# Symmetric attention on one core: the blocks below the diagonal of the diagonal pairs go through VectorE and DRAM, and the diagonal pair moves to the end of its row

## The chip, the core and the metric

The kernel runs on one core of one Trainium2 chip. TensorE (PE in the profile), VectorE (DVE), ScalarE (ACT), GpSimd (POOL) and SyncE (SP, which here only issues DMAs) each work through a list of instructions in order, and 16 DMA engines move data between on-chip memory (SBUF) and DRAM. The metric is the device time of one execution in microseconds.

## What is computed

Layer 0 is attention over the 4096 positions of an image, per batch of four, with 128 channels. `q` is both query and key, and it is scaled by its norms, so the matrix of energies is symmetric:

```python
xs = x.reshape(B, C, h, R, w, R).transpose(0, 1, 3, 5, 2, 4).reshape(B, C * R * R, h, w)
q = xs.reshape(B, C * R * R, hw)                    # 4 x 128 x 4096
energy = jnp.einsum('bci,bcj->bij', q, q)
d = jnp.sqrt(jnp.diagonal(energy, axis1=1, axis2=2))
energy = energy / (d[:, :, None] * d[:, None, :])   # symmetric
attn = jax.nn.softmax(energy, axis=-1)
out = jnp.einsum('bcj,bij->bci', q, attn)
x = gamma * out + xs
```

Layer 1 works on tokens of 128 values: layer norm and a linear attention of 8 heads added to the tokens, then a layer norm, a router, and the two best of 8 experts for each token, added again. Everything is float32.

## The kernel before

**Rows, pairs and blocks.** `attend(b, st)` (L394) does layer 0 of one batch. The 4096 positions are NCH = 8 chunks of CH = 512, each of NJ = 4 blocks of 128. Row `i` takes chunk `i` against the chunks `jc <= i`; this is one pair (jc, i). The order inside a row is written out at L408: the diagonal pair (i, i) first, then 0 to i-1. Only the very last row of the last batch (called `ending`) has another order, and there two pairs are computed twice rather than transposed.

**One tick.** Each block `j` of a pair is a tick: a matmul makes a 128x512 tile `pe` of energies (L510), ScalarE makes `pr = exp(pe)` and the sums of its rows (L513), and two ticks later `values` (L417) multiplies `pr` by the values `qT` and accumulates into the row's one PSUM bank `po`, which ScalarE copies to `o` when the row is complete (L422). The helper `after(n, f)` puts a piece of work n ticks later in every queue.

**The other triangle.** Because exp(energy) is symmetric, the pair (jc, i) also serves chunk jc. For `jc < i` VectorE transposes each `pr` in 32x32 blocks into a tile `F` (L368 in the profile, which is the place where `turn_tick` calls the queued work). `move` (L447) writes `F` to DRAM with one DMA of 1 MB, `bring` (L465) reads it back three ticks later with four DMAs of 256 KB into `G`, in an order that finishes the transposition, and puts `transposed_share` (L370) on the list `late`. From `LAG` = 57 units of the hand-written clock later on, one step of the oldest item is taken per tick (`step_share`): a matmul of `G` into a PSUM bank `pg` (L374), and a ScalarE copy into `junk` for the sums (L379). After four steps VectorE adds `pg` to `o[jc]` (L384). There are three `F`, three `G` and two `pg` buffers.

**The diagonal pair.** For `jc == i` only the blocks on and above the diagonal are computed, so block j has 512-128j columns. The six 128x128 blocks below the diagonal are made by `below` (L425): TensorE transposes three blocks in each of two groups into a PSUM bank `ptd` (L443), ScalarE copies them to `gd` with their sums (L433, three copies), and three further `values` matmuls of 256, 128 and 384 columns go into `po`.

**Order of all other work.** `clock[0]` advances by 8 units for a full tick (two per 128 columns for a narrower one) and by 4 for a step of `late`. Work of other stages is woven in by this clock. The list `timed` holds the preparation of the next batch's chunks (`prep`, L283: input DMAs, TensorE transposes, norms) between given percentages of a batch's clock, which is `UNITS` (L1254). The list `steady` holds layer 1 of the batch (`layer1`), which starts at 84% of its batch and then advances one step per `PACE` = 10 units through the next batch. `close_rows` (L627) begins layer 1 of two chunks when `missing()` says that all their shares have been added. In layer 1, tokens are sorted by expert with indirect DMAs on the POOL queue (`xs<-xn`, L935), multiplied (L995), and gathered again (`yb<-ys`, L1060). SP issues nearly all other DMAs, in order: `blocks<-F` (L460), `G<-blocks` (L468), the loads and stores of layer 1 (L959, L981, L1042), and the inputs (L280).

Of the kernel before, what the change touches and what calls it, by code (L numbers as in the profile page):

```python
# [12 lines left out]
F32 = mybir.dt.float32  # L13
# [3 lines left out]
ALU = mybir.AluOpType  # L17
# [5 lines left out]
def kernel(  # L23
# [10 lines left out]
    expert_b: bass.AP,  # L34
    out: bass.AP,
):

# [242 lines left out]
    def prep(b, kc, st):  # L283

        if b == 0:
            if kc == 0:
                st["all"] = big1.tile([P, 4, 8, HW2, 2], F32, tag="T", name="xx_0")
            xx = st["all"][:, kc]
        else:
            xx = xin.tile([P, 8, HW2, 2], F32, tag="xx", name=f"xx_{b}_{kc}")  # L290
        first = b == 0 and kc == 0
        load_tokens(
            xx.rearrange("p k w r -> p k (w r)"), b, 8 * kc, 8, (nc.sync, nc.scalar if first else nc.sync)
        )
        qT = qpool.tile([P, 2, NJ, P], F32, tag="qT", name=f"qT_{b}_{kc}")
        st.setdefault("qT", {})[2 * kc] = qT[:, 0]
        st["qT"][2 * kc + 1] = qT[:, 1]
        yield
        yield
        yield from idle(1)  # L300

        def load_half(g, pt):
            nc.vector.tensor_copy(
                qT[:, :, 2 * g : 2 * g + 2, :].rearrange("p s j (r c) -> p (j r) s c", c=64),
                pt.rearrange("p (m s c) -> p m s c", s=2, c=64),
            )

        for g in range(2):
            yield
            pt, done = hold(f"ptq_{b}_{kc}_{g}", partial(load_half, g))  # L310
            for jj in range(2):
                for r2 in range(2):
                    k = 4 * g + 2 * jj
                    nc.tensor.transpose(
                        pt[:, ts(2 * jj + r2, P)], xx[:, k : k + 2, :, r2].rearrange("p k w -> p (k w)"), ident
                    )
            yield
            done()
        yield
        yield  # L320
        ss = stat.tile([P, 2 * NJ], F32, tag="ss", name=f"ss_{b}_{kc}")
        rn = stat.tile([P, 2 * NJ, 1], F32, tag="rn", name=f"rn_{b}_{kc}")
        for s in range(2):
            sq = work.tile([P, NJ, P], F32, tag="qs", name=f"sq_{b}_{kc}_{s}", bufs=2)
            nc.vector.tensor_tensor(sq, qT[:, s], qT[:, s], ALU.mult)
            nc.vector.tensor_reduce(ss[:, ts(s, NJ)], sq, AX.X, ALU.add)  # L326
            if first:
                pow_neg_half(rn[:, ts(s, NJ), 0], ss[:, ts(s, NJ)])
            elif s == 1:
                pow_neg_half(rn[:, :, 0], ss)  # L330
            yield
            yield
        yield from idle(1)
        if first:
            keep_running(22, ps_g, "pg")
        scaled = []
        for s in range(2):
            qs = work.tile([P, NJ, P], F32, tag="qs", name=f"qs_{b}_{kc}_{s}", bufs=2)
            nc.vector.tensor_tensor(qs, qT[:, s], rn[:, ts(s, NJ)].to_broadcast([P, NJ, P]), ALU.mult)
            scaled.append(qs)  # L340
        for s, qs in enumerate(scaled):
            yield
            qn = npool.tile([P, CH], F32, tag="qn", name=f"qn_{b}_{2 * kc + s}")
            st.setdefault("qn", {})[2 * kc + s] = qn
            pt, done = hold(f"ptn_{b}_{kc}_{s}", lambda p, qn=qn: nc.scalar.activation(qn, p, AF.Copy))
            for j in range(NJ):
                nc.tensor.transpose(pt[:, ts(j, P)], qs[:, j, :], ident)
            yield
            done()
        yield  # L350
        yield
# [5 lines left out]
    LAG = 57  # L357
    exps = []

    def after(ticks, f):  # L360
        queued.append((tick[0] + ticks, f))

# [7 lines left out]
    def transposed_share(b, st, i, jc, G):  # L370

        pg = ps_g.tile([P, CH], F32, tag="pg", name=f"pg_{b}_{i}_{jc}")
        for ib in range(NJ):
# [11 lines left out]
                st["got"][jc] += 1  # L385
            yield "done" if ib == NJ - 1 else None

    def step_share():
        if late and late[0][0] <= clock[0]:
            clock[0] += NJ  # L390
            if next(late[0][1], "done") == "done":
                late.pop(0)

    def attend(b, st):  # L394
# [10 lines left out]

        for i in range(NCH):
            ending = b == B - 1 and i == NCH - 1
            order = list(range(i - 1)) + [i, i - 1] if ending else [i] + list(range(i))  # L408
            twice = (i - 2, i - 1) if ending else ()
            row = {"left": NJ * (i + 1) + NJ - 1}  # L410

            def values(w, blk, lo, hi, i=i, row=row):
                start = "po" not in row
# [51 lines left out]
            def bring(blocks, i, jc):  # L465
# [4 lines left out]
                    )  # L470
                late.append((clock[0] + LAG, transposed_share(b, st, i, jc, G)))

            def back(w, j, jc, i=i):

                if j == 0:
                    while len(held) > 1:
                        held[0]()
                    banks[0] = 2
                    row["back"] = psum_t(f"back_{b}_{jc}")
                nc.tensor.matmul(row["back"], qT[i][:, j, :], w, start=(j == 0), stop=(j == NJ - 1))  # L480
                if j == NJ - 1:
                    nc.vector.tensor_tensor(st["o"][jc], st["o"][jc], row["back"], ALU.add)
                    st["got"][jc] += 1
                    banks[0] = 3

            for jc in order:
                both = jc in twice
                for j in range(NJ if both else 0):
                    yield
                    tick[0] += 1  # L490
                    pe = ps_e.tile([P, CH], F32, tag="pe", name=f"pe_{b}_back_{jc}_{j}")
                    nc.tensor.matmul(pe, qn[i][:, ts(j, P)], qn[jc], start=True, stop=True)
                    pr = ppool.tile([P, CH], F32, tag="pr", name=f"pr_{b}_back_{jc}_{j}")
                    nc.scalar.activation(pr, pe, AF.Exp, accum_out=sums[:, NJ * i + j, jc : jc + 1])
                    after(2, partial(back, pr, j, jc))
                    turn_tick()
                    clock[0] += 2 * NJ
                    step_share()
                    yield
                if jc < i and not both:  # L500
                    F = fpool.tile([P, 4, NJ, NJ, S], F32, tag="F", name=f"F_{b}_{i}_{jc}")
                    Fb = F.rearrange("p q ib j c -> p ib q j c")
                own = []
                for j in range(NJ):
                    t = NJ * jc + j
                    c0 = 0 if jc < i else P * j
                    yield
                    tick[0] += 1
                    pe = ps_e.tile([P, CH], F32, tag="pe", name=f"pe_{b}_{i}_{t}")
                    nc.tensor.matmul(pe[:, c0:], qn[jc][:, ts(j, P)], qn[i][:, c0:], start=True, stop=True)  # L510
                    pr = ppool.tile([P, CH], F32, tag="pr", name=f"pr_{b}_{i}_{t}")
                    exps[:] = [
                        nc.scalar.activation(pr[:, c0:], pe[:, c0:], AF.Exp, accum_out=sums[:, t, i : i + 1]).ins  # L513
                    ]
                    own.append(pr)
                    if ending and jc == order[-1] and j == NJ - 1:
                        st["exps"] = True
                    after(2, partial(values, pr[:, c0:], t, c0, CH))
                    if jc < i and not both:
                        after(1, partial(nc.vector.transpose, Fb[:, :, :, j, :], pr))  # L520
                        if j == NJ - 1:
                            after(2, partial(move, F, i, jc))
                    elif jc == i and j in (1, 2):

                        after(1 if j == 2 and order[-1] == i else 2, partial(below, own, (2, 1) if j == 1 else (3,)))
                    turn_tick()
                    clock[0] += 2 * (CH - c0) // P
                    step_share()
                    yield
# [20 lines left out]
    def layer1(b, st):  # L550
# [76 lines left out]
        def close_rows(kc):  # L627


            def missing():  # L630
                return len(st["o"]) < 2 * kc + 2 or any(st["got"][c] < NCH - 1 - c for c in (2 * kc, 2 * kc + 1))

            late_rows = alone and kc >= 2
            last_rows = alone and kc == 3
# [616 lines left out]
    ENGINES = {getattr(mybir.EngineType, nm) for nm in ("PE", "DVE", "Activation", "SP")}  # L1251
    PACE = 10
    steady = []
    UNITS = 3 * NJ * NJ * NCH * (NCH - 1) // 2 + 5 * NJ * NCH  # L1254

    first = prep(0, 0, states[0])
    next(first)
# [8 lines left out]
    for b in range(B):  # L1266
# [5 lines left out]
            timed.append((setup_sorting(), 58, 98, 9))  # L1272
        if b + 1 < B:
            nxt = states[b + 1]
            timed.append((prep(b + 1, 0, nxt), 66, 82, 12))
            timed.append((prep(b + 1, 1, nxt), 83, 99, 12))
        timed.append((input_rows(b, states[b]), *((55, 75) if b in (0, B - 1) else (82, 99)), 9))
        done = [0] * len(timed)
        start = clock[0]
# [20 lines left out]
                pass  # L1300
        timed = []
        if b + 1 < B:
            timed.append((prep(b + 1, 2, nxt), 2, 20, 12))
            timed.append((prep(b + 1, 3, nxt), 30, 50, 12))
    for steps, _ in steady:
        for _ in steps:
            pass
# [40 lines left out]
```

## Time and profile before

| what | value |
|---|---|
| median of 3 runs | 1768.3 us (1759.68 to 1770.12) |
| profiled execution, its time | 1764.02 us |
| its span, first to last instruction | 1762.2 us |
| PE busy | 1680.6 us (95%) |
| DVE, ACT, POOL busy | 888.2, 925.7, 511.7 us |
| DMA moved | 330.83 MB, mean 188 GB/s |
| mean granted TensorE clock | 0.986 |

The span ends about 120 us after the last row of attention: from about 1640 us on only layer 1 of the last batch runs. A matmul in float32 appears as two instructions of the same shape, a transposition by TensorE as one. The durations of matmuls are modelled and overlap, so what a matmul occupies of TensorE is read from the distance between the starts of neighbours.

### The profile page before, as it was taken

To read this page: it belongs to the slowest core of one execution; us is meant where nothing else is said; L and a number is where in the kernel's file an instruction comes from. 1 tells how busy PE (TensorE), PEld (TensorE's weight loads), DVE (VectorE), ACT (ScalarE), POOL (GpSimd) and SP (SyncE) were. 2 spreads that over 40 slices of the span, in tenths; PEclk is the share of its full clock that TensorE was granted. 3 is DMA by queue.
4 is the path that set the end of the run, shared out by engine and by line. 5 is a ranking of instruction groups with operands and counts; after the bars stand their busy time and mean duration, and the time that the engine had idled before them with its cause. 6 is when DMAs were issued, how large, how long until landed. Compare 5 with 4: busy or idle time off the path is not lost. (4 is left out here: it accounts for less than half of the span.)

```text
span 1762.2 us, 20912 instructions
## 1 busy us (share of the span) xinstructions
PE 1680.6 (95%) x5644; PEld 897.5 (51%) x5644; DVE 888.2 (50%) x2226; ACT 925.7 (53%) x2893; POOL 511.7 (29%) x553
## 2 busy tenths in 40 slices
PE   8999999999999999889999999899999999987887
PEld 5444544455654555445564455435555455544543
DVE  3333333555584244567367334456638524444686
ACT  4455445466565445356565445436656455534376
POOL 1000000001026504451015632553102660453166
PEclk9999999999999999999999999999999999998989
DMA  3565888755567798895556879998465789993001
GB/s 75 177 178 168 209 210 248 237 133 166 155 203 207 216 251 228 234 251 154 153 173 197 248 199 253 247 242 223 144 178 153 216 252 252 268 254 100 7 13 37
DMA packets 217845, 330.83 MB, mean 188 GB/s; under 512 B 24448, under 2 KB 136576, under 8 KB 203776
## 3 DMA queue, kind: packets, MB, share of 16 engines
q1 hardware_dynamic: 197472, 290.52, 59.1%
q0 software_dynamic: 12288, 25.19, 5.0%
q10 hardware_dynamic: 7968, 13.77, 2.7%
q8 instruction: 47, 0.77, 0.2%
q14 instruction: 70, 0.57, 0.1%
HBM read 171.45 MB, written 160.96 MB: 189 GB/s over the span
## 5 line engine op out<-in xcount | busy, mean ns | idle before, releaser
L513 ACT ACTIVATE pr<-pe 128x512 f32<-128x512 f32 (+1 forms) x576 | 322.8, 561 | 565.2 <-PE pe L510 409.0
L417 PE MATMUL po<-pr,qT 128*128 128x512 f32 (+3 forms) x1152 | 551.7, 561 | 0.5 <-ACT o L422 0.5
L510 PE MATMUL pe<-qn,qn 128*128 128x512 f32 x896 | 463.7, 599 | 6.8 <-ACT pr L513 5.0
L374 PE MATMUL pg<-G,qT 128*128 128x512 f32 x880 | 453.1, 596 | 14.3 <-DMA G<-blocks 8.5
L368 DVE STREAM_TRANSPOSE F<-pr 128x512 f32<-128x512 f32 x440 | 308.5, 705 | 223.6 <-ACT pr L513 202.6
L417 PEld LDWEIGHTS po<-pr,qT 128*128 128x128 f32 x1152 | 217.5, 191 | 242.1 <-issue 230.9
L379 ACT ACTIVATE junk<-G 128x512 bf16<-128x512 f32 x440 | 273.5, 622 | 1.0 <-issue 0.5
L374 PEld LDWEIGHTS pg<-G,qT 128*128 128x128 f32 x880 | 163.7, 192 | 197.3 <-issue 188.0
L1060 POOL DMA_INDIRECT yb<-ys,place x192 | 185.5, 966 | 194.9 <-ACT pr L513 59.0
L935 POOL DMA_INDIRECT xs<-xn,place x192 | 186.3, 970 | 135.0 <-issue 47.7
L510 PEld LDWEIGHTS pe<-qn,qn 128*128 128x128 f32 x896 | 154.6, 192 | 123.0 <-issue 104.7
L384 DVE TENSOR_TENSOR o<-o,pg 128x512 f32<-128x512 f32 x110 | 75.3, 685 | 231.7 <-PE pg L374 161.4
L165 POOL TENSOR_TENSOR rn<-ss,neg_half 128x8 f32<-128x8 f32 (+1 forms) x17 | 26.9, 1584 | 445.5 <-DVE ss L326 386.1
L513 ACT ACTIVATION_READ_ACCUMULATOR pr<-pe 128x1 f32 x576 | 112.5, 195 | 0.0
L969 ACT ACTIVATE xn<-pys 128x256 f32<-128x256 f32 (+1 forms) x120 | 45.1, 379 | 113.7 <-PE pys L1002 74.6
L995 PEld LDWEIGHTS pys<-ew_sb,xn 128*128 128x128 f32 x468 | 69.1, 191 | 61.4 <-issue 45.2
L165 POOL TENSOR_TENSOR rsf<-dm_f,neg_half 128x8 f32<-128x8 f32 (+1 forms) x15 | 26.2, 1748 | 249.9 <-DVE sv_f L584 249.9
L510 PE MATMUL pe<-qn 128*128 128x512 f32 (+3 forms) x256 | 91.1, 438 | 4.9 <-ACT pr L513 4.2
L379 ACT ACTIVATION_READ_ACCUMULATOR junk<-G 128x1 f32 x440 | 84.8, 193 | 0.0
L1029 DVE SCALAR_TENSOR_TENSOR acc<-yb,weight,acc 128x128 f32<-128x128 f32 x192 | 65.4, 343 | 34.8 <-DMA yb<-ys,place 15.4
L165 POOL TENSOR_TENSOR rsa<-dm_a,neg_half 128x8 f32<-128x8 f32 x16 | 26.5, 1656 | 191.3 <-DVE sv_a L584 188.9
L995 PE MATMUL pys<-ew_sb,xn 128*128 x468 | 71.7, 276 | 9.7 <-ACT xn L969 9.7
(183 smaller groups left out, 1561.9 us busy)
## 6 DMA issues: line engine op xcount, KB each, us to landing
blocks<-F SPq DMA_DIRECT2D x108, 1024.0 KB
G<-blocks SPq DMA_DIRECT2D x432, 256.0 KB
xn<-xs SPq DMA_DIRECT2D x114, 128.0 KB
T<-in_x_dram SPq DMA_DIRECT2D x64, 128.0 KB
out_dram<-acc SPq DMA_DIRECT2D x128, 64.0 KB
xx<-in_x_dram SPq DMA_DIRECT2D x62, 128.0 KB
ys<-xn SPq DMA_DIRECT2D x60, 128.0 KB
ys<-result SPq DMA_DIRECT2D x54, 128.0 KB
```

The source lines that it names most:

```text
L165: pinned(nc.gpsimd.tensor_tensor(dst, src, neg_half.to_broadcast(list(src.shape)), ALU.pow))
L368: f()
L374: nc.tensor.matmul(pg.rearrange("p (a f) -> p a f", a=4), st["qT"][i][:, ib, :], G[:, :, ib], start=(ib == 0), stop=(ib == NJ - 1),)
L379: nc.scalar.activation(junk, G[:, :, ib], AF.Copy, accum_out=st["sums"][:, NJ * i + ib, jc : jc + 1])
L384: nc.vector.tensor_tensor(o, o, pg.rearrange("p (a j c) -> p a j c", a=4, c=S), ALU.add)
L417: nc.tensor.matmul(row["po"][:, lo:hi], qT[blk // NJ][:, blk % NJ, :], w, start=start, stop=(row["left"] == 0))
L510: nc.tensor.matmul(pe[:, c0:], qn[jc][:, ts(j, P)], qn[i][:, c0:], start=True, stop=True)
L513: nc.scalar.activation(pr[:, c0:], pe[:, c0:], AF.Exp, accum_out=sums[:, t, i : i + 1]).ins
L935: inst = nc.gpsimd.indirect_dma_start(xs[h], offset(place[:, i, k : k + 1]), xn[:, k, :], None)
L995: nc.tensor.matmul(p[:, 2 * P + j * D : 2 * P + j * D + D], bufs[4 + g % 2][:, j, :], weights[:, bass.ds(begins[2 * (g % 2) + j], D)], sta ...
L1029: nc.vector.scalar_tensor_tensor(a[:, k % 4, :], yb[k // 4][:, i, k % 4, :], weight[:, i, k, :], a[:, k % 4, :], ALU.mult, ALU.add)
L1060: inst = nc.gpsimd.indirect_dma_start(yb[k // 4][:, i, k % 4, :], None, ys, offset(place[:, i, k : k + 1]))
```

## The change

The diagonal pairs lose the TensorE transposes and get the way of all other pairs. For each row but the ending one:

- VectorE transposes each block right of the diagonal by itself (`turn_blocks`, six instructions of 128x128) into an `F` tile of 128 x 768 values.
- `move_diagonal` writes it to DRAM with one DMA (384 KB), `bring_diagonal` reads it into a `G` tile with four (96 KB each), and `diagonal_share` is put on `late`. It has two steps: a matmul of 384 columns, then two of 256 and 128, into a `pg` bank, with three ScalarE copies for the sums, and VectorE adds 128x384 of `pg` to `o[i]`.
- the row's `po` takes only its own 4(i+1) matmuls.
- the diagonal pair is now last in its row.
- `missing()` waits for the diagonal share as well.
- in `prep`, the batches after the first wait one step longer between the input DMA and its first use (13 steps rather than 12), and one start moves from 66% to 65%; `UNITS` counts the diagonal pair as 28 units rather than 20.
- the computed-twice pairs of the ending row also set `exps`, which the indirect DMAs wait for.

```diff
-        yield from idle(1)
+        yield from idle(2 if b else 1)
...
+    BELOW = {1: 0, 2: 1, 3: 3}
...
+    def diagonal_share(b, st, i, G):
+
+        pg = ps_g.tile([P, CH], F32, tag="pg", name=f"pg_{b}_{i}_{i}")
+        out = pg[:, : 3 * P].rearrange("p (a f) -> p a f", a=4)
+        for step in ((3,), (2, 1)):
+            for ib in step:
+                rows = G[:, :, BELOW[ib] : BELOW[ib] + ib, :].rearrange("p a m c -> p a (m c)")
+                nc.tensor.matmul(
+                    out[:, :, : ib * S], st["qT"][i][:, ib, :], rows, start=(ib == 3), stop=(ib == 1)
+                )
+                junk = work.tile([P, 4, 3 * S], BF16, tag="junk", name=f"junk_{b}_{i}_{i}_{ib}", bufs=1)
+                nc.scalar.activation(
+                    junk[:, :, : ib * S], rows, AF.Copy, accum_out=st["sums"][:, NJ * i + ib, NCH:]
+                )
+            if step == (2, 1):
+                o = st["o"][i].rearrange("p (j a c) -> p a j c", a=4, c=S)[:, :, :3]
+                nc.vector.tensor_tensor(
+                    o, o, pg[:, : 3 * P].rearrange("p (a j c) -> p a j c", a=4, c=S), ALU.add
+                )
+                st["got"][i] += 1
+            yield "done" if step == (2, 1) else None
...
-            order = list(range(i - 1)) + [i, i - 1] if ending else [i] + list(range(i))
+            order = list(range(i - 1)) + [i, i - 1] if ending else list(range(i + 1))
             twice = (i - 2, i - 1) if ending else ()
-            row = {"left": NJ * (i + 1) + NJ - 1}
+            row = {"left": NJ * (i + 1) + (NJ - 1 if ending else 0)}
...
+            def move_diagonal(F, i):
+                blocks = dram.tile([4, S, 4, 6 * S], F32, tag="below", name=f"below_{b}_{i}", bufs=4)
+                nc.sync.dma_start(
+                    blocks.rearrange("a p q f -> (a p) q f"), F.rearrange("p q m c -> p q (m c)")
+                )
+                after(3, partial(bring_diagonal, blocks, i))
+
+            def bring_diagonal(blocks, i):
+                G = gpool.tile([P, 4, 6, S], F32, tag="G", name=f"G_{b}_{i}_{i}")
+                for q in range(4):
+                    nc.sync.dma_start(
+                        G[ts(q, S)].rearrange("p a m c -> p a (m c)"), blocks[:, :, q].rearrange("a p f -> p a f")
+                    )
+                late.append((clock[0] + LAG, diagonal_share(b, st, i, G)))
+
+            def turn_blocks(F, pr, j):
+                for ib in range(j + 1, NJ):
+                    nc.vector.transpose(F[:, :, BELOW[ib] + j, :], pr[:, ts(ib, P)])
...
+                elif jc == i and not ending:
+                    F = fpool.tile([P, 4, 6, S], F32, tag="F", name=f"F_{b}_{i}_{i}")
...
+                    elif jc == i and not ending:
+                        if j < NJ - 1:
+                            after(1, partial(turn_blocks, F, pr, j))
+                        if j == NJ - 2:
+                            after(2, partial(move_diagonal, F, i))
...
-                return len(st["o"]) < 2 * kc + 2 or any(st["got"][c] < NCH - 1 - c for c in (2 * kc, 2 * kc + 1))
+                return len(st["o"]) < 2 * kc + 2 or any(
+                    st["got"][c] < NCH - c - (alone and c == NCH - 1) for c in (2 * kc, 2 * kc + 1)
+                )
...
-    UNITS = 3 * NJ * NJ * NCH * (NCH - 1) // 2 + 5 * NJ * NCH
+    UNITS = 3 * NJ * NJ * NCH * (NCH - 1) // 2 + 7 * NJ * NCH
...
-            timed.append((prep(b + 1, 0, nxt), 66, 82, 12))
-            timed.append((prep(b + 1, 1, nxt), 83, 99, 12))
+            timed.append((prep(b + 1, 0, nxt), 65, 82, 13))
+            timed.append((prep(b + 1, 1, nxt), 83, 99, 13))
...
-            timed.append((prep(b + 1, 2, nxt), 2, 20, 12))
-            timed.append((prep(b + 1, 3, nxt), 30, 50, 12))
+            timed.append((prep(b + 1, 2, nxt), 2, 20, 13))
+            timed.append((prep(b + 1, 3, nxt), 30, 50, 13))
```

More of the change, by code (lines that the diff above doesn't have):

```diff
@@ L493, in attend @@
                     pr = ppool.tile([P, CH], F32, tag="pr", name=f"pr_{b}_back_{jc}_{j}")
-                    nc.scalar.activation(pr, pe, AF.Exp, accum_out=sums[:, NJ * i + j, jc : jc + 1])
+                    exps[:] = [
+                        nc.scalar.activation(pr, pe, AF.Exp, accum_out=sums[:, NJ * i + j, jc : jc + 1]).ins
+                    ]
                     after(2, partial(back, pr, j, jc))
```

## The prediction

> **What bounds the kernel now.** I read the page first, for which engine has no slack and where.
>
> ```profile
> PE 1680.6 (95%) x5644; PEld 897.5 (51%) x5644; DVE 888.2 (50%) x2226; ACT 925.7 (53%) x2893; POOL 511.7 (29%) x553
> ...
> PE   8999999999999999889999999899999999987887
> ...
> PEclk9999999999999999999999999999999999998989
> DMA  3565888755567798895556879998465789993001
> ```
>
> PE is full in nearly all slices; DVE and ACT are half idle. But three stretches of the DMA row stand at 9, so there is a second resource to watch. PE's busy time is modelled, so I counted the distances between the starts of neighbouring matmuls in the trace: 429 ns (median) for a pass of 512 columns, 323 for 384, 216 for 256, about 110 for 128. At these distances all 5,644 instructions need about 1627 us; some 122 us are excess, of which 24 us lie after 1640 us (a tail that the change does not touch) and nearly all the rest in a few places: 21 us at 680-800, 19 us at 1080-1200, 23 us at 1560-1640, 6 us at 560-600, 6 us in the first 40 us. Elsewhere PE is back to back, and a matmul less is time less.
>
> Next, the timeline of PE around one diagonal pair (start, duration, instruction):
>
> ```profile
> 100.13 0.81 PE L417 MATMUL po<-pr,qT 128*128 128x384 f32 x2
> 100.78 0.49 PE L443 MATMUL ptd<-ident,pr 128*128 128x128 f32 x3
> 101.11 1.02 PE L374 MATMUL pg<-G,qT 128*128 128x512 f32 x2
> ...
> 103.26 0.49 PE L443 MATMUL ptd<-ident,pr 128*128 128x128 f32 x3
> 103.59 1.02 PE L374 MATMUL pg<-G,qT 128*128 128x512 f32 x2
> ```
>
> Three transpositions hold PE from 100.78 to 101.11 and from 103.26 to 103.59: 0.33 us, 0.11 each, not the 0.275 that their row gives as duration. The groups by form give counts and the prices of the way that replaces them:
>
> ```profile
> L368 DVE STREAM_TRANSPOSE F<-pr 128x512 f32<-128x512 f32 x440 | 308.5, 705 | 223.6 <-ACT pr L513 202.6 <-issue 19.4 <-DMA G<-blocks 0.8
> ...
> L384 DVE TENSOR_TENSOR o<-o,pg 128x512 f32<-128x512 f32 x110 | 75.3, 685 | 231.7 <-PE pg L374 161.4 <-remote 31.1 <-issue 17.2
> ...
> L443 PE MATMUL ptd<-ident,pr 128*128 128x128 f32 x192 | 31.1, 275 | 0.0
> ```
>
> Then the waits of PE (us in total, times, longest), and the busy times by windows, for where extra DMA or DVE work could hurt:
>
> ```profile
> PE ptq L314 <- DMA xx<-in_x_dram: 10.3, 3, 5.6
> ...
> PE pg L374 <- DMA G<-blocks: 8.5, 4, 4.4
> ```
>
> ```profile
> 480.00:520.00 40.00, 39.41 (x122) 19.89 (x121) 33.98 (x127) 25.88 (x76) 8.00 (x12) 1.00 0.53 164
> ...
> 720.00:760.00 40.00, 33.83 (x81) 15.19 (x80) 20.42 (x42) 13.34 (x42) 21.43 (x21) 0.91 0.94 229
> ...
> 880.00:920.00 40.00, 40.00 (x164) 24.35 (x163) 25.29 (x99) 27.14 (x81) 6.31 (x9) 1.00 0.54 165
> ...
> 1160.00:1200.00 40.00, 33.92 (x82) 14.33 (x80) 23.54 (x60) 13.34 (x42) 26.52 (x27) 0.96 0.99 259
> ```
>
> The columns after the width are PE, weight loads, DVE, ACT, POOL, granted clock, DMA share, GB/s. Where the DMA share is about 0.5, PE misses nothing; at 0.94 and 0.99 it loses 6 of 40 us, mostly to a late `G` or a late input, each with a stretch at half clock behind it.
>
> **What the skill says.** The Trainium skill, "TensorE: Matmul & The Clock Gate", Part 4, has a TensorE transposition as a matmul against the identity whose PSUM result must then be copied; the trace agrees (L443, then ACT L433), though the page's 275 to 390 ns is a latency and the stream here pays 110. Its Part 1 says that an idle window of about 3.4 us halves the clock; the trace agrees: after the 4.4 us wait at 747 us four passes in a row start about 853 ns apart. "DMA: Bandwidth & Descriptors", "Issuing engines are not separate DMA queues", says that all queues share the 16 engines, so the new transfers compete with those of layer 1 although SP issues them; the windows above fit that.
>
> **The change part by part.**
>
> *TensorE transposes.* 31 of 32 rows lose six: 186. The 192 take 21.3 us start to start, so 186 take **20.6 us** off PE. They lie in the stretches where PE is back to back, so I take them in full. The three value matmuls of 384, 256 and 128 columns remain as `pg` matmuls: zero.
>
> *ACT.* The copies to `gd` (492, 383, 270 ns, each with a read of its sum) become copies to `junk`. For 512 columns `junk` takes 622 and a PSUM read 596, so under 0.1 us a row: zero, and ACT is at 53%.
>
> *DVE.* Six 128x128 transposes and one 128x384 add a row. No such transpose is in the trace: a quarter of 705 is 176 ns below, the skill's 311 ns ("VectorE: DVE Perf Modes", The three transpose paths, for bf16) above; other 128x128 instructions on DVE take 279 to 343, so I take 0.31. The add takes 0.55 (546 ns, L805 of that size). 6 x 0.31 + 0.55 = 2.4 us a row, 75 us in all, behind PE. In the fullest windows (34 of 40 us, at 480-520, 920-960, 1320-1360) one row of about 50 us adds 2: still under 40. Queued behind are releases of PSUM banks and the transposes into `F`; I charge 2 us (0 to 6).
>
> *DMA.* A row writes 128 packets of 3072 B and reads 512 of 768 B. In the trace the main queue's packets take on average 33 ns (512 B), 144 (2048 B), 170 (4096 B). Between these, 768 B is about 52 and 3072 B about 131: (512 x 52 + 128 x 131)/16 = 2.7 us of all 16 engines a row (1.3 to 6), 84 us in all, some 5% of the span. A pair costs 512 x 144/16 + 128 x 325/16 = 7.2 us in its 10.3 us (four ticks of 2.58), so the diagonal ticks, which moved nothing new, are the troughs it fills. At the sixth and seventh rows, where the share is 0.9, two or three rows a batch find no trough. The `G` there is late by up to 2.7 us more, once, since PE's stall stops the clock of the following ones too: I charge 4 us over three batches (0 to 15).
>
> *SP.* Five more issues a row at 0.35 to 0.45 us, and one more wait for a landing: L468 waits 287.7 us in 66 cases, 4.4 each. Behind it queue layer 1's loads and stores. `G` still has 57 units (five ticks, 12 us) before it is used: zero in quiet stretches; in full ones it is in the 4 us.
>
> *Buffers.* A `G` every four ticks now also at the diagonal; it is held five ticks of LAG and four of use, 9 of the 12 that three buffers allow. `pg`: the share of two ticks lies between others of four; the bank before last is free. `pr` loses a user.
>
> *Order and clock.* With the diagonal last, the bank `po` changes in a full tick instead of a narrow one, so the copy to `o` has 1.7 us of PE work as cover; the two waits of 0.4 us at 23.7 and 38.2 us vanish. A batch counts 28x48+8x28 = 1568 units instead of 1504, so layer 1 takes six more steps in it and reaches the last row some 15 us earlier; there the gather of the previous batch meets the loads of `T`. Less of a collision, perhaps; unmeasured: -10 to +5 us, taken at 0.
>
> *prep.* One step more, 20 units or 4.4 us, before the input is used. Of the three `ptq` waits one is the start (5.6 us); the others, 1.7 and 3.0 us at 722 and 1144, are shorter than that, and the second has 1.7 us of half clock behind it. They could fall away: 6 us; but the same DMA backlog makes the next `G` late, so I take **4 us** (0 to 7).
>
> Sum: -20.6 - 4 + 2 + 4 = **-21 us** (rounded). Against the profiled execution, 1764.0 (span 1762.2 and 1.8 around it), that is 1743; the median, 4.3 above it, gives **1747**.
>
> **Rivals.** *Busy stretches eat the gain.* For: the 0.94 and 0.99 shares, and that every stall there costs half clock behind it. Against: only two or three of eight diagonals fall there. At the upper ends (DMA 15, DVE 6, prep 0): -20.6 + 21 = 0, and a middle of -8: 1760.
> *Slower: the exchanges are exposed.* If a diagonal's DMA finds no trough at all, it costs PE its 2.7 us; eight of 31 exposed use up the 20.6 us, fifteen make the kernel 20 us slower, all 31 give 84 - 21 = +63. For fifteen: 1788. Rows 5 to 7 of each batch, 12 of 32, lie in stretches with a share of about 0.75 or more; against it, that share is an average in which the diagonal ticks themselves are empty.
> *Better: collisions clear.* The layer's earlier steps and the later use of `xx` free the stretches at 720-800, 1120-1200 and 1560-1600, which hold about 45 us of stalls: a fourth of it gives 1735.
> *The change does not do what it says:* only the ending row keeps its six transposes; excluded.
>
> **How the numbers follow.** The forecast (1738 to 1754) 0.57, collisions clear 0.08, gain eaten 0.24, exposed 0.11. A measurement of this kernel can tell about 1% (18 us) from no change, and the bound for faster is 1750.6; some 0.07 of the forecast's 0.57 lies above it. Faster 0.58, same 0.31, slower 0.11. The range reaches from the clear case to the end of the eaten one: 1731 to 1769, since nothing below its upper end needs exposed exchanges.
>
> **What would show it.** PE: 6 `ptd` matmuls left, and about 1606 us of starts; quiet windows at full PE; `pg` waits for `G` at 680-800 within 5 us of now; the `ptq` waits gone but the first; DVE near 963 us; DMA 355 MB. Wrong if PE waits for `G` in quiet stretches too (exposed), if DVE's queue delays PSUM banks at 480-520, or if a row's end shows a new wait for `o`.

## The result and the profile after

The changed kernel takes 1757.98 us (median of 20 runs, 1752.69 to 1765.63) against 1766.46 us before (20 runs): ratio 0.9947, 95% interval 0.9932 to 0.9962, which is 9 us faster. The forecast was 1747 us and 21 us. Below, a difference of ratios is turned into microseconds with 1766 us. The profiled execution has a span of 1751.4 us. The page of the changed kernel first:

```profile
PE 1667.8 (95%) x5458; PEld 882.2 (50%) x5458; DVE 939.7 (54%) x2443; ACT 927.0 (53%) x2893; POOL 512.0 (29%) x553
...
PE   8999998999999999899999999979999999899887
...
PEclk9999999999999999999999999989999999999989
DMA  4675877776568799997567799998656889995001
```

The 186 transposes are gone (5458 instructions for 5644). With the same distances between starts as in the prediction, the matmuls need 1606.9 us instead of 1627.1: TensorE was given 20.2 us less to do, as forecast. But its stalls (what the starts are apart beyond these distances) went from 121.9 to 131.0 us. The profiled execution is one of 20, which spread over 13 us, so a difference of 2 or 3 us between two traces says little. By stretches:

| stretch, us | before | after | without the diagonals' trip to DRAM (run below) |
|---|---|---|---|
| 0-160 | 5.9 | 7.1 | 7.1 |
| 160-290, batch 0 | 3.0 | 17.8 | 6.1 |
| 290-680 | 9.9 | 9.7 | 9.1 |
| 680-800 | 21.0 | 17.2 | 16.8 |
| 800-1090 | 6.8 | 8.9 | 11.5 |
| 1090-1225 | 18.8 | 20.9 | 18.0 |
| 1225-1480 | 6.2 | 6.6 | 10.4 |
| 1480-1640 | 25.8 | 18.4 | 13.9 |
| from 1640 | 24.4 | 24.5 | 19.3 |

The PE digits say the same: the sixth and seventh, at 220-308 us, are 9 and 9 before and 9 and 8 after. The waits of PE in the changed kernel (us in total, times, longest):

```profile
PE pg L375 <- DMA G<-blocks: 25.6, 11, 6.3
...
PE ptq L313 <- DMA xx<-in_x_dram: 5.7, 1, 5.7
...
PE po L440 <- ACT o L445: 3.5, 14, 0.5
```

The first line has the waits for the `G` of ordinary pairs (`G<-blocks`), not of the diagonals (`G<-below`), for which PE has no wait in the list. Two of the three waits for the input are gone, and a small wait for `o` at the end of rows is new: 3.5 us in 14, before 0.5 in 2.

The list holds only the waits whose last releaser the profile names as a `G`. The groups give all idle time before the matmuls that read a pair's `G`, in the changed kernel, in the kernel before, and in the run without the trip:

```profile
L375 PE MATMUL pg<-G,qT 128*128 128x512 f32 x880 | 456.8, 601 | 37.5 <-DMA G<-blocks 25.6 <-issue 7.0 <-DVE rdx L699 2.4
```

```profile
L374 PE MATMUL pg<-G,qT 128*128 128x512 f32 x880 | 453.1, 596 | 14.3 <-DMA G<-blocks 8.5 <-issue 5.8
```

```profile
L375 PE MATMUL pg<-G,qT 128*128 128x512 f32 x880 | 451.9, 595 | 25.1 <-DMA G<-blocks 7.9
```

So PE waits 37.5 us here against 14.3 before. The DMA packets of the traces say whose waits these are: in 14 of the 15 here, 7 of 8 before and all 13 without the trip, the last packet of the `G` landed within 1.4 us before the matmul began, so PE took it up as it came. Nearly all are late `G`, also where the profile names DVE or nobody. The windows (columns as in the prediction), the last line from the kernel before in a fence of its own:

```profile
160.00:290.00 130.00, 120.36 (x320) 57.16 (x319) 43.79 (x78) 55.75 (x178) 0.00 (x0) 0.96 0.76 204
480.00:520.00 40.00, 39.36 (x128) 20.64 (x127) 33.81 (x128) 27.90 (x84) 9.90 (x13) 1.00 0.68 189
...
720.00:760.00 40.00, 32.62 (x71) 14.03 (x70) 19.86 (x44) 13.88 (x42) 23.91 (x25) 0.87 0.99 253
1160.00:1200.00 40.00, 33.71 (x91) 15.70 (x90) 24.22 (x62) 17.70 (x52) 18.66 (x18) 0.87 0.94 242
```

```profile
160.00:290.00 130.00, 130.00 (x369) 63.28 (x368) 45.85 (x73) 64.24 (x203) 1.64 (x1) 1.00 0.81 215
```

DVE's window at 480-520 us did not suffer. The two stretches in which the prediction saw danger lose about what they lost. PE's new loss is at 160-290 us, where it was full before and where the mean DMA share is no higher than then (0.76 and 0.81). How one such loss arises, in the timeline of SP's queue (start, duration with the waits between its DMAs) and of PE, both of the changed kernel:

```profile
250.29 0.37 SPq L483 DMA_DIRECT2D blocks<-F  x1
251.01 3.74 SPq L279 DMA_DIRECT2D T<-in_x_dram  x4
254.79 9.80 SPq L279 DMA_DIRECT2D xx<-in_x_dram  x4
264.71 1.81 SPq L491 DMA_DIRECT2D G<-blocks  x4
```

```profile
265.21 1.02 PE L440 MATMUL po<-pr,qT 128*128 128x512 f32 x2
272.26 2.04 PE L375 MATMUL pg<-G,qT 128*128 128x512 f32 x2 [6.03 <-DMA G<-blocks]
274.10 1.06 PE L313 MATMUL ptq<-ident,xx 128*128 128x128 f32 x4
```

SP needs 13.6 us to issue eight input loads of 128 KB. Of these, 8 us are waits of the third and the fourth load of `xx` (2.2 and 5.9): in the trace the DMAs of SP's queue carry eight semaphores in turn, and one goes out only when the earlier DMA with its semaphore has landed. The read of `G`, next in its queue, goes out at 264.7 us, 14.4 us after the write; for the pair before this one 4.0 us lay between them (244.51 and 248.46). PE arrives at 266 us and waits to 272.3, and the passes behind start about 853 ns apart, half clock. In the kernel before, the read of the same `G` was late too:

```profile
248.91 0.34 SPq L460 DMA_DIRECT2D blocks<-F  x1
259.18 1.79 SPq L280 DMA_DIRECT2D xx<-in_x_dram  x4
261.14 1.75 SPq L468 DMA_DIRECT2D G<-blocks  x4
```

There it went out 12.2 us after its write, but PE came for this `G` only at 271.7 us, 3.4 us after its last packet. Now the read leaves 3.6 us later and PE comes 5.5 us earlier: PE has saved time, and the transfers have not. SP's own waits show how much less room its queue has (changed kernel, then before):

```profile
SPq L506 <- DMA below<-F: 134.3, 28, 6.9
SPq L483 <- DVE F L369: 91.5, 29, 6.5
```

```profile
SPq L460 <- DVE F L368: 254.0, 36, 28.7
```

Before, SP spent 254.0 us waiting for DVE to finish the next `F`, which is time that its queue had to spare. Now this is 91.5 us, and 134.3 us go to waiting for the diagonals' writes to land. The waits for one of the eight semaphores are no longer in total than before (84 us, 95), though 1233 DMAs now share them, for 1078.

### The profile page after: what moved, and what is told of

Same layout as the page of the kernel before. It is cut to its first block, busy times and chain, and to the rows that moved or that the text cites. A ratio compares the mean times of both kernels' runs of the same rounds, so it can differ in the third digit from the quotient of the medians.

```text
span 1751.4 us, 21197 instructions
## 1 busy us (share of the span) xinstructions
PE 1667.8 (95%) x5458; PEld 882.2 (50%) x5458; DVE 939.7 (54%) x2443; ACT 927.0 (53%) x2893; POOL 512.0 (29%) x553
## 5 line engine op out<-in xcount | busy, mean ns | idle before, releaser
L375 PE MATMUL pg<-G,qT 128*128 128x512 f32 x880 | 456.8, 601 | 37.5 <-DMA G<-blocks 25.6
L375 PEld LDWEIGHTS pg<-G,qT 128*128 128x128 f32 x880 | 167.3, 192 | 239.6 <-issue 205.8
L559 ACT ACTIVATION_READ_ACCUMULATOR pr<-pe 128x1 f32 x576 | 112.1, 195 | 0.0
L1048 PE MATMUL pys<-ew_sb,xn 128*128 x468 | 71.8, 276 | 11.4 <-ACT xn L1022 5.4
L1031 DVE COPY result<-pys 128x256 f32<-128x256 f32 (+1 forms) x60 | 24.6, 410 | 101.6 <-ACT xn L1022 46.2
```

The lines of the kernel that those rows point to most:

```text
L375: nc.tensor.matmul(pg.rearrange("p (a f) -> p a f", a=4), st["qT"][i][:, ib, :], G[:, :, ib], start=(ib == 0), stop=(ib == NJ - 1),)
L1048: nc.tensor.matmul(p[:, 2 * P + j * D : 2 * P + j * D + D], bufs[4 + g % 2][:, j, :], weights[:, bass.ds(begins[2 * (g % 2) + j], D)], sta ...
```

## The experiments

Each ratio is to the kernel before, on the same chip, with its 95% interval. The theories, as named in the expectations: A, the volume of the diagonals' transfers delays the pairs' `G`; B, their issues and waits on SP delay what is queued behind; C, one-off loads of batch 0 were moved in front of a `G`; D, the order itself costs; E (formed later), the diagonal takes one of three `G` buffers.

**The parts: order, trip, preparation.** First, the kernel before with the diagonal last:

```diff
-            order = list(range(i - 1)) + [i, i - 1] if ending else [i] + list(range(i))
+            order = list(range(i - 1)) + [i, i - 1] if ending else list(range(i + 1))
```

> The kernel before with one part of the change: the diagonal pair is last in its row, TensorE still transposes its blocks. Theories for the missing 11 us. A (volume: the diagonals' own transfers make the G of the pairs late): the order costs nothing, within 3 us of before. B (SP: the added issues and waits for landings hold up other DMAs): the same, within 3 us. C (timing: the clock and the earlier preparation put the loads of batch 0 ahead of a G): the same, within 3 us. D (the order itself costs, at the row's end): 6 to 11 us slower than before.

0.9972 (0.9956 to 0.9989). The order is worth 5 us by itself; D falls. Where the 5 us come from isn't shown: its profiled execution, at 1769 us above its median, has no smaller stalls (127.0 us). PE waits for no `G` there, but longer for `pr` (18.5 us, before 9.3) and for the input (18.7, before 10.3). Next, the changed kernel without the trip:

```diff
-                blocks = dram.tile([4, S, 4, 6 * S], F32, tag="below", name=f"below_{b}_{i}", bufs=4)
-                nc.sync.dma_start(
-                    blocks.rearrange("a p q f -> (a p) q f"), F.rearrange("p q m c -> p q (m c)")
-                )
...
-                    nc.sync.dma_start(
-                        G[ts(q, S)].rearrange("p a m c -> p a (m c)"), blocks[:, :, q].rearrange("a p f -> p a f")
-                    )
-                late.append((clock[0] + LAG, diagonal_share(b, st, i, G)))
+                late.append((clock[0] + LAG, diagonal_share(b, st, i, None)))
...
-                rows = G[:, :, BELOW[ib] : BELOW[ib] + ib, :].rearrange("p a m c -> p a (m c)")
+                rows = ident[:, None, : ib * S].to_broadcast([P, 4, ib * S])
```

> The changed kernel without the way through DRAM of the diagonal blocks: VectorE transposes as before, but nothing is written to or read from DRAM and the share multiplies the identity instead (this leaves out those values). A (volume) and B (SP) both expect the full 20 us: ratio to before about 0.988. C (timing) and D (order) expect it to stay near the changed kernel, 0.994 to 0.996.

0.9848 (0.9818 to 0.9878), 27 us faster than before and 17.5 us faster than the changed kernel. Its waits of PE:

```profile
PE pg L375 <- DMA G<-blocks: 7.9, 7, 2.6
...
PE ptq L313 <- DMA xx<-in_x_dram: 5.7, 1, 5.7
```

The stalls are 112.1 us, 18.9 below the changed kernel, and the two profiled executions lie 19.2 us apart. All else of the change is still there (DVE's transposes, the `pg` matmuls, the `junk` copies, the order, the preparation; the matmuls on the identity start as far apart as those on `G`), so the missing time is the trip's. The late `G` accounts for part of it: the 7.9 us above leave out the waits with another releaser, and all idle time before the pairs' matmuls is 25.1 us (its group is shown above), 12 us less than in the changed kernel but 11 more than before. A further part is half clock. Over all executions the granted clock is 0.987 here and 0.983 in the changed kernel (medians of 6 and 20), which makes about 7 us; this is an estimate, from clock and span. And 5 us of the 19 lie after 1640 us, where no pair is left; what they are isn't shown. SP waits 268.2 us for the next `F` again. Third, the preparation timed as before:

```diff
-        yield from idle(2 if b else 1)
+        yield from idle(1)
-            timed.append((prep(b + 1, 0, nxt), 65, 82, 13))
+            timed.append((prep(b + 1, 0, nxt), 66, 82, 12))
```

The other three get 12 steps as well.

> The changed kernel with the preparation of the next batch timed as before (one step less, 12 steps, 66%). C (timing: the inputs of batch 1 issued right behind those of T at 251 us hold G up by some 8 us with the half clock behind it) expects 5 to 9 us faster than the changed kernel, about 0.990, if the waits for the input do not return; the prediction's term for prep expects those to return, +4 to 6 us. A and B expect +4 to 6 us against the changed kernel, about 0.998.

0.9971 (0.9954 to 0.9988), 4 us slower than the changed kernel. Its waits of PE:

```profile
PE ptq L313 <- DMA xx<-in_x_dram: 24.4, 5, 7.7
PE pg L375 <- DMA G<-blocks: 10.8, 7, 2.2
```

The intervals of the two just overlap, so the 4 us are uncertain. The waits for the input come back and some of those for `G` go (24.9 us of idle time before the pairs' matmuls): 49 us of both here, 43 in the changed kernel. The two partly stand in for each other.

**The trip: volume, SP or buffer.** Small pieces: the same number of DMAs, order and waits, each moving 16 values where 192 were:

```diff
-                    blocks.rearrange("a p q f -> (a p) q f"), F.rearrange("p q m c -> p q (m c)")
+                    blocks.rearrange("a p q f -> (a p) q f")[:, :, :16], F.rearrange("p q m c -> p q (m c)")[:, :, :16]
...
-                        G[ts(q, S)].rearrange("p a m c -> p a (m c)"), blocks[:, :, q].rearrange("a p f -> p a f")
+                        G[ts(q, S)].rearrange("p a m c -> p a (m c)")[:, :, :16], blocks[:, :, q, :16].rearrange("a p f -> p a f")
```

> The changed kernel with the diagonal's way through DRAM kept in number and order of DMAs and in its waits on SP, but with 64 B pieces: each DMA moves 32 KB or 8 KB, a twelfth (the share multiplies the identity; this leaves out the values). Without any trip the ratio was 0.9848, with the whole trip 0.9947. A (volume on the 16 engines delays the pairs' G) expects most of the gap back, 0.985 to 0.988. B (SP's issues and waits for landings hold up what is behind them) expects 0.992 to 0.995. Half and half: 0.990.

0.9898 (0.987 to 0.9927): half of the gap. As in the run without the trip, the share multiplies the identity (this part of the edit isn't shown). Its third `junk` copy reads a small piece of `G`, so that a wait for it stays, on ACT. In bytes the trip is a twelfth, in the time of the DMA engines more: counted in the traces, the 768 B pieces take 45 ns each and the 3072 B pieces 141, 80 us of all 16 engines in total; the 64 B pieces take 12 ns each, 23 us. So it separates less well than its expectation says. Nor does its trace, the slowest of its six executions, show where the gain lies: PE waits as long for the pairs' `G` as in the changed kernel (37.5 us). With a small tile of its own, so that no `G` buffer is taken:

```diff
+    dpool = ctx.enter_context(tc.tile_pool(name="dpool", bufs=2))
...
-                G = gpool.tile([P, 4, 6, S], F32, tag="G", name=f"G_{b}_{i}_{i}")
+                G = dpool.tile([P, 4, 1, 16], F32, tag="Gd", name=f"Gd_{b}_{i}")
```

> The small trip of the run before (64 B pieces, all DMAs and SP waits, the share multiplies the identity, values left out), but the diagonal's pieces land in a small tile of their own and take no G buffer. With the G buffer the ratio was 0.9898, without any trip 0.9848. A new theory E (buffers: the diagonal takes one of three G, so the next pairs' loads wait on SP for one to be read, 22 us in 8 waits for PE's pg in the changed kernel and none before) expects 0.984 to 0.987. B (SP's issues and landing waits) expects it to stay, 0.989 to 0.992.

0.9902 (0.9872 to 0.9933), unchanged: for the small trip E falls, although in the changed kernel SP did wait for buffers. The full trip with a buffer of its own, and with LAG 69, and the control for the `pr` buffers taken for it:

```diff
-    ppool = ctx.enter_context(tc.tile_pool(name="ppool", bufs=6))
+    ppool = ctx.enter_context(tc.tile_pool(name="ppool", bufs=5))
+    dpool = ctx.enter_context(tc.tile_pool(name="dpool", bufs=1))
...
-                G = gpool.tile([P, 4, 6, S], F32, tag="G", name=f"G_{b}_{i}_{i}")
+                G = dpool.tile([P, 4, 6, S], F32, tag="Gd", name=f"Gd_{b}_{i}")
```

> The changed kernel, full trip and values, with a buffer of its own for the diagonal's G (3 KB a partition; the pr buffers go from 6 to 5 to make room). E (buffers) expects about half of the gap to 0.9848 back: 0.988 to 0.991, and no wait of SP for pg on a pair's G. A (volume) and B (SP) expect no change, 0.993 to 0.996.

> The same with LAG 69. If the buffers are what limits a longer lag, this is better than LAG 69 with a shared buffer (0.988): 0.983 to 0.986. If LAG 69 and the own buffer repair the same loss, 0.987 to 0.989.

> Control for the two runs with a buffer of its own: the changed kernel with 5 pr buffers for 6, else the same. A pr lives two ticks, so 5 suffice: no change, 0.993 to 0.997. If it is slower, the two runs with an own buffer are to be read against it.

0.9985 (0.9968 to 1.0003), 0.9949 (0.9926 to 0.9972) and 0.9934 (0.9914 to 0.9954). Five `pr` buffers cost nothing, the own buffer 9 us against that control. It brought a wait of its own, since there is only one; SP's waits in the first of these (us in total, times, longest):

```profile
SPq L507 <- PE pg L397: 26.3, 4, 9.2
```

SP stood up to 9.2 us for the last diagonal to be read, with all its queue behind it. This run therefore does not tell E from B; the small tile above, with two buffers, does so for the small trip. With LAG 69 this wait is 40.4 us, and the run is 12 us slower than LAG 69 with the shared buffers (below).

The read moved away from the landing of the write:

```diff
-                after(3, partial(bring_diagonal, blocks, i))
+                after(5, partial(bring_diagonal, blocks, i))
```

> The changed kernel, where the diagonal's read from DRAM is put on SP five ticks after the write instead of three, so that SP no longer waits for the write to land (134 us in 28 waits now, 4.8 each). B (that wait holds the DMAs behind it) expects half or more of the gap of 17 us back: 0.987 to 0.990. A (volume) expects no change, 0.993 to 0.996.

1.0001 (0.9985 to 1.0018), 9.5 us slower than the changed kernel. SP's wait for this landing shrank from 134.3 us in 28 to 88.0 in 24, and did not go, but the time got worse. The later read brought waits of its own: PE waits 11.4 us for `o` (3.5 in the changed kernel) and 10.4 us for the sorted tokens (`xn<-xs`, none listed there), while the idle time before the pairs' matmuls fell to 28.8 us. So the run gives B no support, but doesn't clear that wait either. The five DMAs on POOL's queue, in full size, then with LAG 69, then in small pieces:

```diff
-                nc.sync.dma_start(
+                nc.gpsimd.dma_start(
                     blocks.rearrange("a p q f -> (a p) q f"), F.rearrange("p q m c -> p q (m c)")
...
-                    nc.sync.dma_start(
+                    nc.gpsimd.dma_start(
                         G[ts(q, S)].rearrange("p a m c -> p a (m c)"), blocks[:, :, q].rearrange("a p f -> p a f")
```

> The changed kernel with the five DMAs of each diagonal on the POOL queue instead of SP's, full size. B (order on SP) expects the half that the small trip left: 0.988 to 0.991. A (volume) alone expects no change, 0.993 to 0.996. If POOL's indirect DMAs now wait behind these, slower than that.

> The same with LAG 69. If the longer lag and the free SP repair the same late G, 0.986 to 0.989, as LAG 69 alone (0.988). If they repair different losses, 0.982 to 0.985.

> The small pieces of 64 B (values left out, the share multiplies the identity) on the POOL queue. If size and SP's order are two parts that add up to the cost of the trip, this is the kernel without any trip: 0.983 to 0.987. If the small pieces already had all that can be had (0.990), the rest is in what every trip keeps, a G buffer and its waits: 0.988 to 0.992.

0.9921 (0.9889 to 0.9952), 0.9873 (0.9843 to 0.9903) and 0.9894 (0.986 to 0.9928). On this queue the full trip takes 78 us of the 16 engines, 80 on SP's. In the first of these, batch 0 is nearly whole again with the full volume; its window:

```profile
160.00:290.00 130.00, 127.04 (x348) 60.62 (x347) 49.65 (x88) 61.84 (x197) 7.18 (x11) 1.00 0.82 228
```

The stalls there are 6.8 us, against 17.8 with the same DMAs on SP. The other runs agree: PE is busy for 127.4 of the 130 us in both other runs on POOL, full with LAG 69 or in small pieces, and for 127.6 without the trip, but for 120.4 in the changed kernel, 119.9 in its control with five `pr` buffers, and 123.7 and 123.8 with small pieces on SP. In that place it is SP's queue.

But the time gains only 4.6 us on the changed kernel, inside both intervals, and small pieces on POOL are no better than small pieces on SP. The traces show why the sum doesn't come out: the pairs' `G` are hardly later than without the trip (25.0 us of idle time against 25.1), but PE has a new wait, in the first and the third of these runs:

```profile
PE pe L556 <- ACT pr L559: 15.5, 9, 4.1
```

```profile
PE pe L557 <- ACT pr L560: 16.2, 9, 3.6
```

It is 1.6 us in the changed kernel, 2.1 and 3.0 with small pieces on SP, and 4.3 without the trip; its longest cases come once a batch, near 558, 976 and 1394 us in the first of these runs. So moving the DMAs to POOL exchanges one wait for another, and these runs don't tell what the trip costs without SP's order. What ends the new wait isn't shown; the profile has ACT waiting there for something that it can't name, while POOL issues its indirect DMAs.

**Where in time.** In batch 0 the next inputs, and then also the weights, later:

```diff
-            timed.append((prep(b + 1, 0, nxt), 65, 82, 13))
+            timed.append((prep(b + 1, 0, nxt), 65 if b else 70, 82, 13))
...
-            timed.append((setup_weights(), 46, 58, 9))
+            timed.append((setup_weights(), 49, 61, 9))
```

> The changed kernel, in batch 0 alone the preparation of the next batch starts at 70% instead of 65%, so its input loads no longer follow directly on those of T. C (bunched one-off loads of batch 0 hold a G: 10.6 us of stall at 240-280 against 0.1 before) expects 5 to 9 us better: 0.990 to 0.992. A and B (spread over all rows) expect no change, 0.993 to 0.996.

> The same, and the loads of the weights in batch 0 start at 49% instead of 46%, after the G they delayed at 167-188 us. C expects another 3 to 4 us from it: 0.988 to 0.990. A and B expect no change, 0.993 to 0.996. If the weights then meet the next G instead, the same as the run with the inputs alone.

0.9941 (0.992 to 0.9962) and 0.9911 (0.9881 to 0.9941). The first gives nothing that can be told, the second 6 us at the edge of the intervals; the stalls at 160-290 us are 13.8 and 12.5. The first speaks against C; the interval of the second holds most of what C expected (0.988 to 0.990) and part of what A and B did (0.993 to 0.996), so for the two loads together it stays open.

**A longer lag.** `LAG` decides how long a `G` has to land:

```diff
-    LAG = 57
+    LAG = 69
```

> The changed kernel with LAG 69 for 57, so each G has one tick (2.6 us) more to land. All theories that end in a late G (A, B, C): of the 11 waits for G, 25.6 us in total with half clocks behind them, those below 2.6 us vanish and the others shorten: 5 to 12 us faster than the changed kernel, about 0.988 to 0.992. D (order) expects no change, 0.9947. If three G buffers are then too few, it is slower.

> The kernel before with LAG 69 for 57. It waits for a late G only 4 times, 8.5 us. If the 12 us that LAG 69 gave the changed kernel repair what the change broke, it gives the kernel before at most 2 to 4 us, 0.998 to 1.000. If LAG 57 was too short for both kernels alike, it gives some 10 us here too, 0.994, and the change with LAG 69 is then no better against this than the change was against before.

> No trip (values left out, as in the run without a trip at 0.9848) and LAG 69. If LAG 69 repairs only the lateness that the trips bring, no change: 0.984 to 0.986. If it repairs a lateness that is there without them, as the 7 us in the kernel before suggest, 0.979 to 0.982.

> The changed kernel with LAG 81, two ticks more than 57. If lateness of G is the whole loss and three buffers suffice, a little better than LAG 69 (0.988): 0.984 to 0.987. If a G is then held so long (seven ticks of lag and four of use, of the 12 that three buffers give) that the next load starts late, no better than LAG 69 or worse: 0.988 to 0.995.

In the changed kernel 0.988 (0.9849 to 0.991), in the kernel before 0.996 (0.9945 to 0.9976), without the trip 0.9764 (0.9726 to 0.9801): 12, 7 and 15 us. So `G` comes late in all of them, and the lag repairs a lateness that the trip did not bring: the idle time before the pairs' matmuls falls from 37.5 to 23.1 us, from 14.3 to 0.4, and from 25.1 to 15.8. The trip still costs 20 us at LAG 69 (0.988 against 0.9764), and the change still gains 14 us (0.988 against 0.996). LAG 81 gives 1.000 (0.9987 to 1.0014). SP's waits in that run:

```profile
SPq L491 <- PE pg L375: 90.2, 20, 10.6
```

In the changed kernel this wait, for a `G` buffer to be read, is 14.1 us in 7: now three buffers are too few, and the loads start late. The changed kernel with LAG 69, one number changed, beats both kernels; with POOL's queue it is as good (0.9873), not better by what the intervals can tell.

## Why the prediction was wrong

The direction was right, the size was not. The outcome is where the rival in which the gain is eaten had put it (0.24, at 1760 us), but by other terms: that rival lost prep's gain and paid for DVE, and neither happened. The sum itself has a slip: its terms, -20.6 - 4 + 2 + 4, give -18.6 and not -21, so the forecast should have been 1749 us. That is 2 of the 12 us missing.

- *TensorE transposes, -20.6.* Right: 20.2 us in the starts.
- *ACT, zero.* Right: 927.0 against 925.7 us.
- *DVE, 75 us behind PE, 2 charged.* Harmless, and smaller: 52 us. The group of the new transposes by form:

```profile
L513 DVE STREAM_TRANSPOSE F<-pr 128x128 f32<-128x128 f32 x186 | 44.0, 283 | 22.9 <-ACT pr L559 22.2 <-issue 0.7
```

  283 ns lie between the two ends taken (176 and 311), and one after the other they overlap: 186 are busy for 44.0 us, 0.24 each. PE's stall at 480-520 us stayed (1.8 and 1.6).
- *prep, -4.* Right as far as can be told: undoing it costs 4 us, with intervals that just overlap, and the waits for the input return.
- *Order, 0.* It gives 5 us in the kernel before. The two waits for `o` that should vanish became 14, 3.5 us in all: a sign that the prediction named, and small.
- *DMA, 4 us charged (0 to 15), and SP, zero "in quiet stretches".* This is the step that failed. The load itself was well sized: 2.7 us of the engines a row were forecast, 80 us over 31 rows are 2.6. What failed is the exposure: the trip costs 17.5 us instead of 4 and zero, a fifth of its engine time. With this, an estimate from the measured parts comes near the result: -20.2 - 4 - 5 + 17.5 is -12 us, measured -9. And the place was wrong: "At the sixth and seventh rows, where the share is 0.9" PE loses what it lost, while 12 of the 19 us of stall that vanish without the trip lie at 160-290 us of batch 0, with a share of 0.8 and hardly a stall before (3.0 us): the prediction's own sign of exposed exchanges, in one stretch. SP's five issues and one landing a row were put at zero there, because `G` had five ticks; the runs on POOL's queue show that this loss is SP's queue. The margin, from the last packet of a `G` to its first matmul, was thin there in places without showing, since a `G` that lands just in time makes no wait: of the ten `G` used at 160-290 us before, three had 3.4 us or less and the others 6.4 to 14.1. Over all 110 the median was 10.5 us; it is 7.8 after the change, and 8.2 without the trip, so most of the lost margin isn't the trip's; PE's own saving could be the cause, but no run shows it.
- *Half clock behind each stall.* Too strong: of the waits for `G` listed before, those at 746.9 and 1167.9 us (4.43 and 2.18 us) have passes 853 ns apart behind them, those at 776.1 and 1195.6 (0.75 and 1.12) have not. The 2.18 us are also shorter than the 3.4 us that the prediction goes by.
- *Buffers, 9 of 12 ticks.* Not the cause as far as the small trip tells, but tighter than thought: SP waits for them, and two ticks more are too many.

What is shown: the trip costs 17.5 us; at 160-290 us, where 12 of the 19 us of stall lie, it costs through a late `G` of the pairs, and SP's queue makes it late. What stays open: what in SP's queue does it, the issues, the waits for the diagonals' writes or those for a semaphore, and how the rest divides. Small pieces return half on either queue without a shorter wait for `G` on SP's, and the runs on POOL's queue have the wait for `pr` in place of what they save.

## What to carry to other kernels

A transfer for which no engine waits may still have little margin, and taking work from the engine that waits for it uses up margin too. Before adding to a queue, look at how early the data lands, and at what stands ahead of it in the issuing queue at each moment, not only at the mean share of the DMA engines and at the waits. When adding up waits, take all that stand before the reading instruction: the list by releaser showed 7.9 us of late `G` without the trip, and it was 25.1. A price of a transfer in engine time and its price in the time of the kernel are different things; here a fifth of one became the other, in single collisions, some with half clock behind them. Lengthening the prefetch by one step gave the changed kernel 12 us, more than the change itself, and nothing when it was lengthened by two.

## What the hardware showed beyond expectation

VectorE's transposes of 128x128, issued in a row, overlap: five took 1.07 us though each is recorded with about 283 ns (changed kernel):

```profile
137.79 1.07 DVE L513 STREAM_TRANSPOSE F<-pr 128x128 f32<-128x128 f32 x5
```

And pieces of 64 B take 12 ns of a DMA engine, a quarter of the 45 ns of pieces of 768 B, for a twelfth of the data; cutting a transfer's bytes by twelve cut its engine time by 3.4.
